# A transformer block: q, k and v of the second batch in seven block products for two token tiles, with weight sums kept from the first batch

## Chip, cores, metric

One core of a Trainium2 chip runs the whole program. The metric is device time in microseconds; the median of three runs of the kernel before is 3139.4 us.

## What is computed

One conditioned transformer block on `x` of 2 x 2048 x 576 in float32, 16 heads of 36, an MLP of 2304. A condition gives shifts, scales and gates. The change is in the lines that make q, k and v.

```python
mod = silu(c) @ w_ada + b_ada            # shifts, scales, gates
xn = ln(x, 1e-06) * (1 + sc_msa) + sh_msa
qkv = (xn @ w_qkv + b_qkv).reshape(B, N, 3, H, hd)
q, k = ln(q, 1e-05, qn_g, qn_b), ln(k, 1e-05, kn_g, kn_b)
attn = softmax(q @ k.T * hd ** -0.5)
x = x + g_msa * ((attn @ v) @ w_proj + b_proj)
xn2 = ln(x, 1e-06) * (1 + sc_mlp) + sh_mlp
x = x + g_mlp * (gelu(xn2 @ w1 + b1) @ w2 + b2)
```

## The kernel before

The two batches run one after the other: q, k, v of a batch, its attention, its output projection; the MLP of both stands last. A batch has 16 token tiles of 128 rows. A product on TensorE takes a tile's features as the stationary operand (128 x 128) and half of the columns of q, k or v (288) as the moving one. The 576 features are four full parts in float32 and a last part of 64, which is split into two rounded halves that lie one above the other and is multiplied in the faster fp32r form (the tail). Thus `product` (L1101, L1103) issues, per half, four f32 matmuls and two tail matmuls; the trace shows each f32 matmul as two records. A PSUM tile of pool `s` has two banks, one per half; there are four.

Around a tile's product, per batch, stand these steps:

- POOL loads a tile's rows (L984); DVE and ACT normalise them (L272 to L283, the root `std` L276 on ACT); DVE turns squares of 32 x 32 (L1000), and POOL stores them in four DMAs to a DRAM tile `turned` (L1005).
- POOL loads a tile's features back by column: `xnt` (L1013) and twice the last part (L1015). ACT scales and shifts them: four parts (L1022), the rounded last part (L388), the same unrounded as `tail` (L389); POOL subtracts (L390).
- DVE adds the bias while it empties PSUM (`biased`, L1115 for q and k, L1118 for v). ACT squares q and k (L1055), DVE sums by head (`var`, L1060), ACT takes the root (L1063), DVE inverts (L1065), POOL multiplies (`head_scale`, L1067).
- DVE turns q and k (L1080), and four DMAs write them by feature to DRAM `qk` (L1082, on SP's queue, near the end of a batch also on POOL's).
- For attention, key and query rows come back from `qk` (L812 `km`, L814 `ke`), and DVE scales and splits them (L847, L856, L857). Attention's products are L1245 and L1258, its exponential is L1249 on ACT.

On TensorE, DVE, POOL and SP instructions run in the order in which they are written in this part of the code; the order on ACT is made by a scheduler when the program is built. Every engine's queue is in order: an instruction that waits holds all behind it.

The first batch also makes the weights (`first_weights`): q's and k's columns are centred by head on DVE, the last 64 rows are split, and at tile `TPB + 1` `kept` stores them to DRAM on SP's queue, from where the second batch loads them (`kept_weights`).

## Time and profile before

| what | us |
|---|---|
| median of three runs (3139.19 to 3139.5) | 3139.4 |
| profiled execution, first to last instruction | 3137.1 |
| TensorE busy in it | 3113.8 |
| q, k, v of the second batch on TensorE | 1083.3 to 1295.07 |
| mean granted TensorE clock | 0.999 |

The profile is of one execution; for its own time the page gives the span alone, 2.3 us under the median of the runs. PE is TensorE, PEld its weight loads; DVE, ACT and POOL are the vector, scalar and GpSimd engines, SP the queue that mostly issues DMAs. A group's row names line, engine, operation, tiles and count, then total busy us and mean ns of one, then idle time ahead and what ended it. In a timeline row come start and length in us, and in brackets idle time and releaser. A windows row has the stretch, then busy us per engine with counts, then the granted clock, the DMA engines' share and GB/s.

### The profile page before, as it was taken

Reading aid. Unit: us, or ns where it says so; the run is one execution under the profiler, and the core shown is the slowest. Engines: PE = TensorE matmul, PEld = TensorE weight load, DVE = VectorE, ACT = ScalarE, POOL = GpSimd, SP = SyncE. Lnnn points to the kernel's source line nnn. Section 1 sums busy time; section 2 is a strip of 40 time slices with the busy share of each in tenths; the row PEclk is TensorE's granted clock in tenths of the full one; section 3 lists DMA queues with packets and bytes.
Section 4 is the critical chain, followed back from the end, with each engine's and each line's share of the span. In section 5 each row is a group of like instructions: output and inputs, shape, how many; then the busy total and the mean of one; then the engine's idle time right before and its main releaser. Section 6 shows DMA issues by size and latency. Waiting matters only on the chain.

```text
span 3137.1 us, 46798 instructions
## 1 busy us (share of the span) xinstructions
PE 3113.8 (99%) x17553; PEld 1859.8 (59%) x17553; DVE 1517.1 (48%) x2189; ACT 1472.4 (47%) x2847; POOL 664.8 (21%) x934
## 2 busy tenths in 40 slices
PE   8999999999999999999999999999999999999999
PEld 6883333333334788633333333368888888777777
DVE  6653434443444556444434444345565554545454
ACT  2326666666666132466666666633555541000000
POOL 4640000011110455200011210013333320111111
PEclk9999999999999999999999999999999999999999
DMA  5753221132221756411122321146554434333331
GB/s 147 178 106 85 78 66 46 56 82 68 66 73 53 239 101 123 86 44 35 47 57 73 86 66 56 57 167 191 159 142 132 128 110 166 106 121 121 113 106 39
DMA packets 300707, 311.94 MB, mean 99 GB/s; under 512 B 179192, under 2 KB 233336, under 8 KB 298360
## 3 DMA queue, kind: packets, MB, share of 16 engines
q1 hardware_dynamic: 252496, 192.19, 21.4%
q0 software_dynamic: 44432, 111.07, 13.4%
q10 hardware_dynamic: 3544, 5.60, 0.5%
q8 instruction: 141, 2.31, 0.3%
q14 instruction: 94, 0.77, 0.1%
HBM read 191.80 MB, written 106.45 MB: 95 GB/s over the span
## 4 chain that ended last, share of the span: by engine, by line
PE 98%; DVE 0%; issue 0%; DMA 0%; ACT 0%; POOL 0%; POOLq 0%; ACTq 0%
PE b L1258 29%; PE b L1245 20%; PE s L1833 16%; PE s L1101 12%; PE m L1673 12%; PE s L406 4%; PE m L1687 2%; PE one L1673 2%; PE s L1103 2%; PE s L417 0%; DMA xt<-x_dram 0%; PE b L192 0%; ACT xnt L395 0%; POOL x_dram L1400 0%; DVE wb L1602 0%
## 5 line engine op out<-in xcount | busy, mean ns | idle before, releaser
L1249 ACT ACTIVATE pt<-b 128x512 f32<-128x512 f32 x2048 | 1057.1, 609 | 482.0 <-PE b L1258 266.2
L1258 PE MATMUL b<-pt,vt 128*64 128x512 f32 x4096 | 935.0, 598 | 0.0
L1258 PEld LDWEIGHTS b<-pt,vt 128*64 128x64 f32 x4096 | 271.8, 136 | 582.1 <-issue 438.2
L1245 PE MATMUL b<-qm,km 32*128 32x512 f32 x4096 | 562.6, 613 | 0.0
L1310 DVE TENSOR_TENSOR ot<-b,ot 128x512 f32<-128x512 f32 x192 | 132.7, 691 | 618.6 <-PE b L1258 618.6
L1245 PE MATMUL b<-qe,ke 16*128 16x512 f32 x2048 | 419.3, 791 | 0.0
L1101 PE MATMUL s<-wq,xnt 128*128 128x288 f32 x1536 | 404.9, 407 | 2.0 <-ACT xnt L395 2.0
L1833 PE MATMUL s<-ws,as 128*128 128x288 f32 x1440 | 351.8, 406 | 0.0
L1245 PEld LDWEIGHTS b<-qm,km 32*128 32x128 f32 x4096 | 189.9, 184 | 270.7 <-ACT pt L1249 209.8
L1101 PEld LDWEIGHTS s<-wq,xnt 128*128 128x128 f32 x1536 | 281.7, 190 | 64.6 <-ACT xnt L395 1.6
L1833 PEld LDWEIGHTS s<-ws,as 128*128 128x128 f32 x1440 | 273.6, 190 | 75.6
L1277 DVE RECIPROCAL den<-den 128x512 f32<-128x512 f32 x64 | 213.6, 3337 | 10.6 <-DMA den<-den_dram 10.6
L1673 PE MATMUL m<-xnt,wb 128*128 128x256 f32 x864 | 210.3, 379 | 1.6 <-issue 0.9
L1673 PE MATMUL m<-s,wb 128*128 128x256 f32 x864 | 210.0, 379 | 0.0
L1005 POOL DMA_DIRECT2D turned<-squares x212 | 142.5, 679 | 261.3 <-DVE squares L1000 244.3
L1308 DVE COPY ot<-b 128x512 f32<-128x512 f32 x64 | 44.3, 691 | 278.2 <-PE b L1258 272.9
L1673 PEld LDWEIGHTS m<-s,wb 128*128 128x128 f32 x864 | 164.2, 190 | 22.3
L1245 PEld LDWEIGHTS b<-qe,ke 16*128 16x128 f32 x2048 | 106.1, 184 | 114.1 <-issue 113.4
L1673 PEld LDWEIGHTS m<-xnt,wb 128*128 128x128 f32 x864 | 158.9, 190 | 21.2 <-issue 1.3
L1711 ACT ACTIVATE cs<-cs,b_sb 128x512 f32<-128x512 f32 x144 | 98.8, 719 | 113.1 <-DVE cs L1706 88.7
L812 POOL DMA_DIRECT2D km<-qk x56 | 28.2, 503 | 571.7 <-PE b L1245 569.3
L1022 ACT ACTIVATE xnt<-xnt,mod 128x128 f32<-128x128 f32 x244 | 100.4, 481 | 98.9 <-DMA xnt<-turned 98.8
(206 smaller groups left out, 2942.1 us busy)
## 6 DMA issues: line engine op xcount, KB each, us to landing
gelu<-cs SPq DMA_DIRECT2D x144, 256.0 KB
hidden<-gelu SPq DMA_DIRECT2D x16, 2304.0 KB
x_dram<-spare POOLq DMA_DIRECT2D x64, 288.0 KB, 2.5
qm<-qk SPq DMA_DIRECT2D x256, 64.0 KB
den<-den_dram SPq DMA_DIRECT2D x128, 128.0 KB
turned<-squares POOLq DMA_DIRECT2D x212, 72.0 KB, 2.5
qk<-turned_qk SPq DMA_DIRECT2D x104, 144.0 KB
xnt<-turned POOLq DMA_DIRECT2D x54, 256.0 KB, 4.3
```

The source lines that it names most:

```text
L406: nc.tensor.matmul(outs[a], stationary(k, a), moving(k, a), start=(first and k == 0), stop=(not first and k == FULL - 1),)
L1005: queue.dma_start(out=by_square[g], in_=squares[g * SQ : (g + 1) * SQ, :].rearrange("p (k j) -> p k j", j=SQ))
L1022: nc.scalar.activation(part, part, AF.Identity, **affine(which, k, b))
L1101: nc.tensor.matmul(out_a, full[:, k, :], wq[:, k, f], start=k == 0, stop=False)
L1245: nc.tensor.matmul(ps, k[r, keys], q[r, :], start=first, stop=not first)
L1249: nc.scalar.activation(pt[:, h, :], banks[2 * c + h], AF.Exp, scale=SCALE)
L1258: nc.tensor.matmul(acc[64 * h : 64 * h + 64, :], vt[:, v0 : v0 + 64], pt[:, h, :], start=pt is pts[0][0], stop=pt is pts[-1][0],)
L1277: nc.vector.reciprocal(den, den)
L1310: nc.vector.tensor_tensor(ot, acc, ot, ALU.add)
L1673: nc.tensor.matmul(out_m[m], wb[:, slot[m], k, f * P : (f + 1) * P], moving[m](k), start=k == 0 and m in (1, 2, 5, 6), stop=k == 1 and m == 1,
L1711: nc.scalar.activation(part, part, AF.Gelu, bias=b1_sb[:, g : g + 1])
L1833: nc.tensor.matmul(ms[m], stationary[m][:, f, :], ws[m][:, f, :], start=(f == 0), stop=(f == HF - 1))
```

## The change

For the second batch, from its third tile on, two tiles (`t0`, `t0 + 1`) are multiplied together. Their features by two halves of the first 512 form a 2 x 2 block matrix, and so do the weights by two halves of the inputs and two of the columns; seven block products of sums replace eight. TensorE gets them in four groups, one PSUM tile each: a = (1), b = (2, 6), c = (5, 7), d = (4, 3). The tails stay eight; two matmuls of rows of ones with rows of bias (L1223) bring the bias in. ACT copies the first product to SBUF as `one` (L1233), and DVE makes the results in five additions that also empty PSUM (L1246 to L1250). POOL makes the three sums of the tokens' features with four additions (`token_sums`, L1260 to L1263). The four sums of weights and the difference of the two halves of the last rows are made on DVE in the first batch, one step per tile from the tile after `kept` on, stored by SP's queue, and loaded by it at the start of the second batch. The first two tiles of the second batch are done as before. Both tiles' features are now asked for together, once per pair, and the writing order of the whole stage is new (`in_pairs`).

Lines of the same steps in the new program: product L1136/L1138, bias L1150/L1153, row load L1013, stores L1034, feature loads L1042/L1044, modulation L1051, squares L1090, head scale L1095 to L1102, turned q and k L1115/L1117, attention's products L1489.

**ACT in the middle of the loop.** Before, for one tile and the next (`sq` squares, `var` and `std` roots, `xnt` modulations):

```order
L1063 ACTIVATE var_9611<-var_9611,eps5_67 128x32 [waits DVE_49]
L1055 ACTIVATE sq_9649<-both_9591 128x1152 [waits Activation_49]
L276 ACTIVATE std_9698<-mv_9696,eps6_65 128x1 [waits DVE_49]
L1022 ACTIVATE xnt_9659<-xnt_9659,mod_91 128x128 [waits DMASW6_49,PE_49]
L1022 ACTIVATE xnt_9659<-xnt_9659,mod_91 128x128 x3
L388 ACTIVATE xnt4_9660<-xnt4_9660,mod_91 128x128 [waits DMASW7_49,DMASW0_49,PE_49]
L389 ACTIVATE tail_9661<-xnt4_9660,mod_91 128x128 [waits Pool_49]
L1063 ACTIVATE var_9711<-var_9711,eps5_67 128x32 [waits DVE_49]
L1055 ACTIVATE sq_9745<-both_9691 128x1152 [waits Activation_49]
```

After, for one pair (`one` is the copy of a first product: of k, then q, then v):

```order
L1233 COPY one_9607<-s_9579 128x288 [waits PE_49]
L1098 ACTIVATE var_9560<-var_9560,eps5_67 128x32 [waits DVE_49]
L276 ACTIVATE std_9614<-mv_9612,eps6_65 128x1 [waits DVE_49]
L1051 ACTIVATE xnt_9567<-xnt_9567,mod_91 128x128 [waits DMASW3_49,Pool_49]
L1051 ACTIVATE xnt_9567<-xnt_9567,mod_91 128x128 x3
L388 ACTIVATE xnt4_9568<-xnt4_9568,mod_91 128x128 [waits DMASW5_49,DMASW4_49]
L389 ACTIVATE tail_9569<-xnt4_9568,mod_91 128x128 [waits Pool_49]
L1051 ACTIVATE xnt_9573<-xnt_9573,mod_91 128x128 [waits DMASW6_49]
L1051 ACTIVATE xnt_9573<-xnt_9573,mod_91 128x128 x3
L388 ACTIVATE xnt4_9574<-xnt4_9574,mod_91 128x128 [waits DMASW7_49,DMASW0_49]
L389 ACTIVATE tail_9575<-xnt4_9574,mod_91 128x128
L1233 COPY one_9697<-s_9669 128x288 [waits PE_49]
```

The modulations of two tiles stand in a row, and the copy of q's first product stands behind them. On POOL, the loads that these modulations wait for now stand behind both multiplies of the pair before:

```order
L1102 TENSOR_TENSOR pair_9359<-pair_9359,inv_9552 128x1152 [waits DVE_49]
L1102 TENSOR_TENSOR pair_9359<-pair_9359,inv_9563 128x1152 [waits DVE_49]
L1042 DMA xnt_9567<-turned25_9420 128x4x128 [waits DMASW4_49,DMASW3_49,PE_49]
L1044 DMA xnt4_9568<-turned25_9420 64x128 [waits PE_49]
L1044 DMA xnt4_9568<-turned25_9420 64x128 [waits DMASW5_49]
L1042 DMA xnt_9573<-turned26_9503 128x4x128 [waits DMASW7_49,DMASW6_49,DMASW0_49]
L1044 DMA xnt4_9574<-turned26_9503 64x128 x2
```

where before each tile's loads stood behind the multiply of one tile and the next row load:

```order
L1067 TENSOR_TENSOR both_9691<-both_9691,inv_9810 128x1152 [waits DVE_49]
L390 TENSOR_TENSOR xnt4_9756<-tail_9757,xnt4_9756 128x128 [waits DMASW7_49,DMASW0_49,Activation_49]
L984 DMA xt0_211<-in_x_dram 128x576 [waits DMASW5_49]
L1013 DMA xnt_9843<-turned29_9801 128x4x128 [waits DMASW3_49,DMASW4_49,DMASW2_49,DMASW6_49,DMASW1_49,PE_49]
L1015 DMA xnt4_9844<-turned29_9801 64x128 [waits PE_49,Pool_49]
L1015 DMA xnt4_9844<-turned29_9801 64x128
```

What moved: one multiply and the loads of one tile became two multiplies, then the loads of two tiles.

**TensorE in the same pair**, q's product; its third group is `s_9680`:

```order
L1221 MATMUL s_9669<-wq_8772,xnt_9360 128x288 [waits DVE_49,PE_49]
L1221 MATMUL s_9669<-wq_8772,xnt_9360 128x288
L1223 MATMUL s_9669<-bias_rows_9228,ones_9229 128x288
L1221 MATMUL s_9673<-wq_8772,xnt_9360 128x288 [waits DVE_49]
L1221 MATMUL s_9673<-wq_8772,xnt_9360 128x288
L1227 MATMUL s_9673<-wq4_8773,xnt4_9361 128x288 x2
L1221 MATMUL s_9673<-weight_sums_9147,more_9486 128x288 x2
L1221 MATMUL s_9680<-weight_sums_9147,more_9486 128x288 [waits Activation_49]
L1221 MATMUL s_9680<-weight_sums_9147,more_9486 128x288
L1223 MATMUL s_9680<-bias_rows_9228,ones_9229 128x288
```

The wait on Activation ahead of the third group is for the copy of the first one, whose PSUM tile it takes. Before, a product and the start of the next were:

```order
L1101 MATMUL s_9862<-wq_8754,xnt_9659 128x288 [waits DVE_49]
L1101 MATMUL s_9862<-wq_8754,xnt_9659 128x288 x3
L1103 MATMUL s_9862<-wq4_8755,xnt4_9660 128x288 x2
L1101 MATMUL s_9862<-wq_8754,xnt_9659 128x288 x4
L1103 MATMUL s_9862<-wq4_8755,xnt4_9660 128x288 x2
L1101 MATMUL s_9901<-wq_8754,xnt_9659 128x288 [waits DVE_49]
```

Nothing on TensorE waited for ACT there but for the features.

**POOL at the end of the stage.** Before (`km`, `ke` key rows; `qk` writes; the multiplies are of k of the last tile, then of q of the last two):

```order
L1067 TENSOR_TENSOR both_10443<-both_10443,inv_10460 128x576 [waits DVE_49,Pool_49]
L1082 DMA qk1_9128<-turned_qk_10466 32x18x32 [waits DVE_49]
L1082 DMA qk1_9128<-turned_qk_10466 32x18x32 x3
L1067 TENSOR_TENSOR both_10427<-both_10427,inv_10496 128x576 [waits DVE_49]
L1067 TENSOR_TENSOR both_10443<-both_10443,inv_10524 128x576 [waits DVE_49]
L812 DMA km1_10557<-qk1_9128 32x1024 [waits DMAHW4_49,DMAHW3_49,DMAHW5_49,DMAHW2_49,DMAHW6_49,DMAHW1_49,DMAHW7_49,DMAHW0_49,PE_49]
L814 DMA ke1_220<-qk1_9128 16x1x1024 [waits DMASW5_49]
```

After:

```order
L812 DMA km1_10765<-qk1_9146 32x1024 [waits DMAHW4_49,DMAHW3_49,DMAHW5_49,DMAHW2_49,DMAHW6_49,DMAHW1_49,DMAHW7_49,DMAHW0_49,PE_49]
L814 DMA ke1_220<-qk1_9146 16x1x1024
L812 DMA km1_10765<-qk1_9146 32x1024
L814 DMA ke1_220<-qk1_9146 16x1x1024
L1117 DMA qk1_9146<-turned_qk_10673 32x18x32 [waits DVE_49]
L1117 DMA qk1_9146<-turned_qk_10673 32x18x32 x3
L1102 TENSOR_TENSOR pair_10565<-pair_10565,inv_10723 128x576 [waits DVE_49]
L1102 TENSOR_TENSOR pair_10565<-pair_10565,inv_10730 128x576 [waits DVE_49]
```

Four key loads, which wait for the last v product, moved ahead of the writes and of both multiplies of q.

The diff's core:

```diff
+            def sum_made(i):
+                for k in range(2):
+                    one, other = (
+                        (block(0, 1), block(0, 0)),
+                        (block(1, 1), sums[:, 0]),
+                        (block(1, 1), block(0, 1)),
+                        (sums[:, 1], block(1, 0)),
+                    )[i]
+                    nc.vector.tensor_tensor(sums[:, i, k], one[:, k], other[:, k], ALU.subtract)
...
+            def sums_kept():
+                saved["sums"] = dram.tile([P, 4, 2, 3, HALF], F32, name="sums_kept")
...
-                turned_qk = work.tile([P, 2 * C], F32, name="turned_qk", bufs=3)
+                turned_qk = work.tile([P, 2 * C], F32, name="turned_qk", bufs=3 - b)
...
+                nc.gpsimd.memset(ones[0:2, :].bitcast(F32), 1.0)
...
+                factors = {
+                    1: (a11, by_block(0, 0)),
+                    2: (a12, by_block(1, 0)),
+                    3: (more[:, 2], by_block(1, 1)),
+                    4: (a22, by_sum(3)),
+                    5: (more[:, 0], by_sum(0)),
+                    6: (more[:, 1], by_sum(1)),
+                    7: (s3, by_sum(2)),
+                }
+                tails = {2: (0, tail(0)), 3: (0, tail(1)), 4: (1, less[:, w, :]), 7: (1, tail(1))}
+                out = {}
+                for group in ((1,), (2, 6), (5, 7), (4, 3)):
+                    ps = s_tile()
+                    for a, m in enumerate(group):
+                        out[m] = ps[:, a, :HALF]
+                        out[group] = ps[:, :, :HALF]
+                        x_, w_ = factors[m]
+                        for k in range(2):
+                            nc.tensor.matmul(out[m], x_[:, k, :], w_(k), start=k == 0, stop=k == 1 and m == 6)
+                        if m in (1, 5):
+                            nc.tensor.matmul(out[m], ones, spread[:, w, int(m == 5), :], start=False, stop=True)
+                        if m in tails:
+                            i, w_ = tails[m]
+                            for j in range(2):
+                                nc.tensor.matmul(out[m], parts[i][:, j, :], w_, start=False, stop=j == 1)
...
+                one = work.tile([P, HALF], F32, name="one", bufs=2)
+                nc.scalar.copy(one, out[1])
...
+                tt = nc.vector.tensor_tensor
+                return [
+                    lambda: tt(dst(both_t, 0), two(out[2, 6]), spread_over(single(one)), ALU.add),
+                    lambda: tt(dst(both_t, 1), two(out[5, 7]), spread_over(dst(1, 0)), ALU.add),
+                    lambda: tt(dst(1, 0), dst(1, 1), single(out[4]), ALU.subtract),
+                    lambda: tt(dst(1, 1), dst(1, 1), single(out[5]), ALU.add),
+                    lambda: tt(dst(0, 1), dst(0, 1), single(out[3]), ALU.add),
+                ]
...
+            def token_sums(t0):
+                a, c = xnts[t0][0], xnts[t0 + 1][0]
+                more = work.tile([P, 3, 2, P], F32, name="more", bufs=2)
+                tt = nc.gpsimd.tensor_tensor
+                tt(more[:, 0], c[:, 0:2, :], c[:, 2:4, :], ALU.add)
+                tt(more[:, 1], more[:, 0], a[:, 0:2, :], ALU.subtract)
+                tt(c[:, 0:2, :], a[:, 0:2, :], c[:, 0:2, :], ALU.subtract)
+                tt(more[:, 2], a[:, 2:4, :], more[:, 1], ALU.subtract)
+                return more
+            def row_begun(t):
...
+                    xnts[t] = input_loaded(turned.pop(t), nc.gpsimd, work if t % 4 == 3 else None)
...
+            def in_pairs():
+                sums = work.tile([P, 4, 2, 3, HALF], F32, name="weight_sums")
+                less = work.tile([P, 3, HALF], F32R, name="wq4_less")
+                nc.sync.dma_start(out=sums, in_=saved["sums"])
+                nc.sync.dma_start(out=less.bitcast(F32), in_=saved["less"])
+                row_begun(4)
+                row_begun(5)
+                pairs[0] = work.tile([P, 2, 2 * C], F32, name="pair", bufs=2)
+                both.update((t, pairs[0][:, t, :]) for t in range(2))
+                for t in range(2):
+                    input_modulated(b, xnts[t + 1])
+                    features_begun(t + 2) if t + 2 not in xnts else None
+                    q, k = product(0, t), product(1, t)
+                    biased(0, q, t)
+                    turn_begun(t + 3)
+                    biased(1, k, t)
+                    if t == 1:
+                        turn_begun(5)
+                        row_begun(6)
+                        row_begun(7)
+                    if t > 0:
+                        head_scale(t - 1)
+                    v = product(2, t)
+                    biased(2, v, t)
+                    squared(t)
+                    if t == 0:
+                        spread, ones = bias_rows()
+                input_modulated(b, xnts[3])
+                more = token_sums(2)
+                for t0 in range(2, NT, 2):
+                    last = t0 == NT - 2
+                    operands = sums, less, spread, ones, more
+                    pairs[t0] = work.tile([P, 2, 2 * C], F32, name="pair", bufs=2)
+                    for t in range(2):
+                        both[t0 + t] = pairs[t0][:, t, :]
+                        features_begun(t0 + 2 + t)
+                    out = seven_products(1, t0, operands)
+                    do = combined(1, t0, out)
+                    if t0 == 2:
+                        head_scale(1)
+                    turn_begun(t0 + 4)
+                    do[0]()
+                    by_feature(t0 - 2, ready=not last)
+                    do[1]()
+                    by_feature(t0 - 1, ready=not last)
+                    do[2](), do[3](), do[4]()
+                    if not last:
+                        for t in range(2):
+                            input_modulated(b, xnts[t0 + 2 + t])
+                    if last:
+                        squared(t0, 1, 2)
+                        squared(t0 + 1, 1, 2)
+                    out = seven_products(0, t0, operands)
+                    do = combined(0, t0, out)
+                    if not last:
+                        more = token_sums(t0 + 2)
+                        turn_begun(t0 + 5)
+                        row_begun(t0 + 6)
+                        row_begun(t0 + 7)
+                        for i in range(5):
+                            do[i]()
+                        squared(t0)
+                        out = seven_products(2, t0, operands)
+                        do = combined(2, t0, out)
+                        do[0]()
+                        do[1]()
+                        head_scale(t0)
+                        squared(t0 + 1)
+                        do[2](), do[3](), do[4]()
+                        head_scale(t0 + 1)
+                        continue
+                    head_scale(t0, 1, 2)
+                    do[0]()
+                    head_scale(t0 + 1, 1, 2)
+                    do[1]()
+                    by_feature(t0, 1, 2, ready=False)
+                    do[2](), do[3](), do[4]()
+                    by_feature(t0 + 1, 1, 2, ready=False, queue=nc.gpsimd)
+                    for t in range(2):
+                        squared(t0 + t, 0, 1)
+                    key_rows = [*taken]
+                    for ready in key_rows[:-2]:
+                        ready()
+                    out = seven_products(2, t0, operands)
+                    do = combined(2, t0, out)
+                    head_scale(t0, 0, 1)
+                    do[0]()
+                    head_scale(t0 + 1, 0, 1)
+                    do[1]()
+                    by_feature(t0, 0, 1, ready=False)
+                    do[2](), do[3](), do[4]()
+                    by_feature(t0 + 1, 0, 1, ready=False)
+                    return key_rows[-2:]
...
+            if b > 0:
+                return in_pairs()
...
+                if b == 0 and t > TPB + 1 and summed:
+                    summed.pop(0)()
```

More of the change, by code (lines that the diff above doesn't have):

```diff
@@ L966, in kept @@
                 nc.sync.dma_start(out=saved["wq4"], in_=wq4.bitcast(F32))
-            return (wq, wq4, bq), close, (made, ends_made, bias_made, bias_spread, kept)
+            summed = [*(lambda i=i: sum_made(i) for i in range(4)), ends_less, sums_kept]
+            return (wq, wq4, bq), close, (made, ends_made, bias_made, bias_spread, kept, summed)
         def kept_weights():
@@ L1141, in inputs @@
             if b == 0:
[L1142 removed]
+                made, ends_made, bias_made, bias_spread, kept, summed = making
                 done, modulated = 3, {0, 1, 2}
```

76 lines of the change are left out of this document (68 added, 8 removed).

## The prediction

> **What bounds the kernel now.** I read the page first (busy shares, the chain that ended last), then the stretch in which the second batch's q, k and v are made: its groups of instructions and its table by windows.
>
> ```profile
> PE 3113.8 (99%) x17553; PEld 1859.8 (59%) x17553; DVE 1517.1 (48%) x2189; ACT 1472.4 (47%) x2847; POOL 664.8 (21%) x934
> PE 98%; DVE 0%; issue 0%; DMA 0%; ACT 0%; POOL 0%; POOLq 0%; ACTq 0%
> ...
> L1101 PE MATMUL s<-wq,xnt 128*128 128x288 f32 x768 | 201.9, 406 | 0.0
> L1103 PE MATMUL s<-wq,xnt 128*128 128x288 f32 x192 | 61.7, 402 | 0.0
> ...
> 1120.00:1160.00 40.00, 40.00 (x184) 32.34 (x182) 23.20 (x37) 12.16 (x27) 23.07 (x31) 1.00 0.60 114
> ```
>
> TensorE is 98% of the chain. The two rows in the middle are all of the stage (1083.3 to 1295.07 us): 96 half products, each of 8 records of the f32 lines (two records make one matmul) and 2 of the tail line. TensorE waits for nothing there, so 211.8 / 96 = 2.205 us for a half product. In the windows row TensorE is busy all 40 us, DVE 23.2, ACT 12.2, POOL 23.1. So matmuls taken out are time taken out, as long as what must be made per pair keeps to the shorter beat.
>
> **What is removed and added on TensorE.** A pure f32 stretch of the MLP gives the f32 price:
>
> ```profile
> 2899.80 16.90 PE L1833 MATMUL s<-ws,as 128*128 128x288 f32 x69
> 2916.53 8.65 PE L1833 MATMUL s<-ws,hidden 128*128 128x288 f32 x35
> 1286.16 2.10 PE L1101 MATMUL s<-wq,xnt 128*128 128x288 f32 x8
> 1287.88 0.64 PE L1103 MATMUL s<-wq,xnt 128*128 128x288 f32 x2
> 1288.36 2.10 PE L1101 MATMUL s<-wq,xnt 128*128 128x288 f32 x8
> ```
>
> 16.73 us / 69 = 0.2425 a record, 0.485 a matmul; a tail matmul is then (2.205 - 8 x 0.2425) / 2 = 0.1325. Two tiles of one of q, k, v take four half products now: 16 f32 and 8 tail matmuls, 8.82 us. The seven products take 14 f32, 8 tail and 2 bias matmuls: 14 x 0.485 + 10 x 0.1325 = 8.12. That saves 0.70, for 3 weights x 7 pairs (the first two tiles stay as they were): **-14.6 us**. The starts of the last three rows would split it otherwise (1.72 / 8 = 0.215, 0.48 / 2 = 0.24), which saves 0.38 x 21 = 8.0. I take the first, since 69 records in a row say more than eight; 8.0 is kept as the other end.
> The four groups of a product, in order: a (first product and bias) 1.10, b 2.21, c 2.34, d 2.47.
>
> **What lies beside.** In the first batch eleven subtractions on DVE over five tiles, two or three for a tile of 6 x 2.205 = 13.2 us; the nearest row (752 ns for 576 elements, below) makes 864 about 1.1, so 2.2 to 3.3 us where DVE has 42% idle: 0. Four MB go out and come back on SP's queue; the sums are needed 2 x 13.2 = 26.5 us after they are asked for, and where they came later they would hide in the wait that comes next: 0. Making the bias rows (eighteen short DVE instructions) stands early in the first of these tiles: 0, its cover being the same.
>
> **The loop of pairs.** Durations:
>
> ```profile
> L1067 POOL TENSOR_TENSOR both<-both,inv 128x1152 f32<-128x1152 f32 x13 | 27.6, 2126 | 14.7 <-DVE inv L1065 14.7
> L1115 DVE TENSOR_TENSOR both<-s,bq 128x576 f32<-128x576 f32 x24 | 18.0, 752 | 29.1 <-PE s L1103 29.1
> L1060 DVE TENSOR_REDUCE var<-sq 128x32 f32<-128x1152 f32 x13 | 17.4, 1339 | 0.0
> L272 DVE BATCH_NORM_STATS2 st<-xt 128x6 f32<-128x288 f32 x14 | 5.7, 445 | 0.0
> L1065 DVE RECIPROCAL inv<-var 128x32 f32<-128x32 f32 x13 | 4.6, 353 | 5.0 <-ACT var L1063 5.0
> L1063 ACT ACTIVATE var<-var,eps 128x32 f32<-128x32 f32 x13 | 4.2, 321 | 45.9 <-DVE var L1060 45.9
> xnt<-turned POOLq DMA_DIRECT2D x11, 256.0 KB, 4.9
> DMA to landing us min/median/max: 3.3/4.3/5.9
> ...
> 1181.81 1.65 ACT L1022 ACTIVATE xnt<-xnt,mod 128x128 f32<-128x128 f32 x4 [6.68 <-DMA xnt<-turned]
> 1183.36 0.48 ACT L388 ACTIVATE xnt<-xnt,mod 128x128 fp32r<-128x128 f32 x1
> 1183.75 0.48 ACT L389 ACTIVATE tail<-xnt,mod 128x128 f32<-128x128 f32 x1
> ```
>
> In the new order, group c of q goes into the PSUM tile that group a of the same product left, and ACT empties it (the copy `one`). That copy stands in ACT's queue behind the twelve modulations of the next two feature tiles; those wait for the feature loads, which POOL issues only behind both head-scale multiplies of the pair before. I count from V, when the v product of the pair before ends. Its group c is ready at V - 2.47; DVE then adds (0.75), reduces (1.34), ACT takes the root (0.32), DVE inverts (0.35), does three single adds (3 x 0.445, by the 288-element row), reduces again (1.34), root and inverse (0.67): V + 3.6, with some 0.3 for hops V + 3.9. POOL multiplies (2.13): V + 6.0. The loads land 4.9 later: V + 10.9. Six modulations took 2.42 us in the last rows, so twelve, at their pitch, 4.75: V + 15.7; the copy (0.5; between 0.48 for 128 elements here and the 0.75 of DVE) V + 16.2. TensorE gets there at V + 8.12 + 1.10 + 2.21 = V + 11.4. **It waits 4.7 us**, in each of the five pairs that have a next one to modulate (tiles 4, 6, 8, 10, 12): **+23.5**. With landings of 3.3 and 5.9 it is 3.1 and 5.7: 15.5 to 28.5. Nothing shortens this by itself, since V of the next pair moves along.
>
> **The first pair.**
>
> ```profile
> L1005 POOL DMA_DIRECT2D turned<-squares x42 | 28.2, 678 | 49.4 <-DVE squares L1000 47.9 <-issue 1.5
> L390 POOL TENSOR_TENSOR xnt<-tail,xnt 128x128 fp32r<-128x128 f32 x12 | 5.5, 458 | 4.2 <-ACT tail L389 4.2
> L1000 DVE STREAM_TRANSPOSE squares<-xt 128x576 f32<-128x576 f32 x7 | 5.4, 778 | 0.2
> L283 DVE TENSOR_SCALAR xt<-xt,mv,rstd 128x576 f32<-128x576 f32 x7 | 4.1, 579 | 0.3
> L984 POOL DMA_DIRECT2D xt<-in_x_dram x6 | 3.8, 633 | 0.0
> L276 ACT ACTIVATE std<-mv,eps 128x1 f32<-128x1 f32 x10 | 2.9, 293 | 48.5 <-DVE mv L274 48.5
> ```
>
> The sums of the first pair's tokens (two adds on POOL before the sixth product can start) stand behind a row tile's way to DRAM, and that row's root stands on ACT behind the copy of this pair's group a. From the end of a: copy 0.5, root 0.29, inverse 0.2, normalise 0.58, transpose 0.78, four stores 2.7, two row loads 1.27, multiply 2.13, tail 0.46, two adds of 256 elements (between 458 ns for 128 and the multiply's; 0.65 each) 1.3: 10.2. TensorE has the second product to do meanwhile, 1.24. **+9.0** (7 if the stores were covered half, 9.5 with hops).
>
> **Into attention.**
>
> ```profile
> 1286.19 2.70 POOL L1082 DMA_DIRECT2D qk<-turned_qk  x4 [4.40 <-DVE turned_qk L1080]
> 1290.11 1.16 POOL L1067 TENSOR_TENSOR both<-both,inv 128x576 f32<-128x576 f32 x1 [1.21 <-DVE inv L1065]
> 1292.78 0.78 DVE L1080 STREAM_TRANSPOSE turned_qk<-both 128x576 f32<-128x576 f32 x1
> 1295.07 0.31 PEld L1245 LDWEIGHTS b<-qm,km 32*128 32x128 f32 x8 [0.17 <-DVE turned_qk L1080]
> 1295.17 0.55 POOL L812 DMA_DIRECT2D km<-qk  x1 [1.11 <-PE s L1103]
> 1295.72 0.62 POOL L814 DMA_DIRECT2D ke<-qk  x1
> 1295.97 0.47 DVE L847 TENSOR_SCALAR km<-km,gb_at 64x256 f32<-64x256 f32 x1
> ```
>
> Now POOL's key loads wait for the last v matmul but stand last. In the new order four of them stand ahead of the four stores and of both q multiplies; the transpose of q waits for the first multiply, and DVE's last adds of v, which free attention's second bank, stand behind it. From the last matmul: 2.34 + 2.70 + 1.16 + 0.78 + 0.445 + 0.47 + 0.445 = 8.3, less the 0.17 there is now: **+8.2**. If DVE ran past the transpose it would be 0.
>
> **The clock.** Seven new gaps may cost more than their length.
>
> ```profile
> 17.61 0.55 PE L230 MATMUL s<-ident,rows 128*128 128x128 f32 x3 [0.64 <-DVE rows L222]
> 19.11 5.81 PE L1101 MATMUL s<-wq,xnt 128*128 128x288 f32 x16 [0.95 <-ACT xnt L395]
> 24.54 0.91 PE L1103 MATMUL s<-wq,xnt 128*128 128x288 f32 x4
> 18.00:20.00 2.00, 1.05 (x5) 0.74 (x4) 1.41 (x10) 1.48 (x4) 1.38 (x5) 0.89 1.05 291
> 20.00:24.00 4.00, 4.00 (x11) 2.89 (x11) 2.48 (x6) 1.23 (x4) 0.98 (x2) 0.63 1.08 371
> ```
>
> Behind gaps of 0.64 and 0.95 us at the start the granted clock falls to 0.89 and 0.63 in these windows, and sixteen records take 5.43 instead of 16 x 0.2425 = 3.88: 1.55 lost. Seven gaps cost between 0 and 10.9. It is one instance, so I take 1 us each: **+7**. The Trainium skill, page "TensorE: Matmul & The Clock Gate", section "Part 1: The HAM clock gate (the "warmup" mystery)", says the gate halves the clock after a whole idle window of about 3.4 us on a free-running grid. By that page a gap of 4.7 us holds a whole window about 4 times in 10, the two long ones always, so that the term would be, as an estimate, about 6; the drop above came behind less idle time than the rule asks for.
>
> **The sum** on the profiled span: 3137.1 - 14.6 + 9.0 + 23.5 + 8.2 + 7 = 3170.2. The median of the runs, 3139.4, lies 2.3 above that span: **3172 us**.
>
> **Rivals.**
> - *POOL's queue does not carry the waits* (faster). If its DMA issues ran beside its multiplies, the feature loads would start at V and be hidden, the first pair would wait 9.0 - 2.7 - 1.27 - 2.13 = 2.9 and attention 8.2 - 5.0 = 3.2: 3139.4 - 14.6 + 6.1 = 3131. It decides from the point where the gaps sum to less than 8.3. Against it: the first row of the transition charges POOL 2.70 for four stores, and key loads follow each other at 0.55. Chance 0.08.
> - *The loop holds, the two single waits stay*: 3139.4 - 14.6 + 17.2 + 2 = 3144, no change that can be told. It needs landings below 0.2 us or the copy ahead of the modulations. 0.05.
> - *The transition is covered*: 3172 - 9 = 3163. DVE would have to be late less than the q multiplies. 0.15.
> - *Longer*: landings of 5.9 and the full clock price, 3172 + 5 + 4 = 3181; the two feature tiles now load in one burst, which speaks for it. With the smaller saving, 3188. 0.20.
> - The forecast itself, 3157 to 3179: 0.52.
>
> 0.2% (6.3 us) is what a measurement of this kernel can tell from no change; from the cases: faster 0.08, within it 0.05, slower 0.87. The range reaches from the shortest landings without the transition's wait and without a clock price (3139.4 - 14.6 + 9.0 + 15.5 = 3149) to the longest with the smaller saving, 3188.
>
> **What would show it.** In the trace after: a product of two tiles 8.1 us long; TensorE idle 4 to 5 us five times, released by ACT's copy, with ACT waiting for the feature loads ahead of it; one idle time of about 9 us at the first pair, released by POOL's sums; one of about 8 at the first attention matmul, released by DVE. Granted clock near 0.5 behind some of them. I am wrong if ACT's copy stands ready at V + 11, or if feature loads start before the second multiply has ended.

## The result, and the profile after

The changed kernel takes 3177.3 us (median of four runs, 3174.57 to 3177.69) beside 3139.45 us for the kernel before on the same chip: ratio 1.0119, 95% interval 1.0105 to 1.0133, 37.9 us slower. Its profiled execution spans 3175.0 us, 2.3 under its median as before. The forecast was 3172 with a range of 3149 to 3188.

The page's line of busy times and instructions:

```profile
PE 3114.0 (98%) x17511; PEld 1857.9 (59%) x17511; DVE 1571.6 (49%) x2277; ACT 1479.8 (47%) x2868; POOL 684.7 (22%) x965
```

TensorE is as busy as before (3113.8) with 42 fewer records. So the work taken out is hidden in this line: matmuls at half clock count as longer busy time (27.6 us of it, see below). The waits of TensorE from 40 to 1345 us show the new ones (what waits, on what, us in total, times, longest):

```profile
PE s L1221 <- ACT one L1233: 16.1, 5, 4.3
PE s L1221 <- POOL more L1261: 9.2, 1, 9.2
PE b L1489 <- issue: 7.3, 1, 7.3
PE s L1136 <- ACT xnt L1051: 4.1, 1, 4.1
```

The timeline of TensorE has their places; the second and third rows are the starts of one and the next weight's product of the same pair:

```profile
1127.27 3.87 PE L1221 MATMUL s<-weight_sums,more 128*128 128x288 f32 x8 [9.15 <-POOL more L1261]
1134.80 1.13 PE L1221 MATMUL s<-wq,xnt 128*128 128x288 f32 x4
1142.91 1.13 PE L1221 MATMUL s<-wq,xnt 128*128 128x288 f32 x4
1165.41 2.29 PE L1221 MATMUL s<-weight_sums,more 128*128 128x288 f32 x4 [2.81 <-ACT one L1233]
...
1283.28 1.37 PE L1221 MATMUL s<-weight_sums,more 128*128 128x288 f32 x4 [4.26 <-ACT one L1233]
1330.76 1.55 PE L1489 MATMUL b<-qm,km 32*128 32x512 f32 x3 [7.26 <-issue]
```

An undisturbed product of two tiles takes 1142.91 - 1134.80 = 8.11 us, as forecast (8.12). The stage now runs from 1089.14 to 1322.38 us, 233.24 us long where it was 211.77. Attention's first two matmuls start at 1322.38 and its third at 1330.76.

POOL ahead of the first pair's sixth product, whose wait ends at 1127.27: a head-scale multiply and, behind it, the second of the token sums.

```profile
1123.19 2.14 POOL L1102 TENSOR_TENSOR pair<-pair,inv 128x1152 f32<-128x1152 f32 x1
...
1126.49 0.72 POOL L1261 TENSOR_TENSOR more<-more,xnt 128x256 f32<-128x256 f32 x1
```

POOL and DVE ahead of attention's third matmul: four stores, the two multiplies of q, then the transpose that waits for the first of them, and the addition whose end (1330.66) lies 0.1 us before that matmul:

```profile
1324.71 2.67 POOL L1117 DMA_DIRECT2D qk<-turned_qk  x4
1327.40 2.27 POOL L1102 TENSOR_TENSOR pair<-pair,inv 128x576 f32<-128x576 f32 x2
1328.60 0.78 DVE L1115 STREAM_TRANSPOSE turned_qk<-pair 128x576 f32<-128x576 f32 x1 [2.67 <-POOL pair L1102]
...
1330.20 0.46 DVE L1249 TENSOR_TENSOR vt<-vt,s 128x288 f32<-128x288 f32 x1
```

One pair of the loop, from the head-scale multiplies of the pair before to the product that waits:

```profile
1243.78 2.13 POOL L1102 TENSOR_TENSOR pair<-pair,inv 128x1152 f32<-128x1152 f32 x1 [1.04 <-DVE inv L1100]
1245.85 0.79 POOL L1042 DMA_DIRECT2D xnt<-turned  x1
...
1249.36 1.65 ACT L1051 ACTIVATE xnt<-xnt,mod 128x128 f32<-128x128 f32 x4 [4.41 <-DMA xnt<-turned]
1253.60 0.48 ACT L389 ACTIVATE tail<-xnt,mod 128x128 f32<-128x128 f32 x1
1253.99 0.38 ACT L1233 COPY one<-s 128x288 f32<-128x288 f32 x1
...
1254.42 1.24 PE L1221 MATMUL s<-weight_sums,more 128*128 128x288 f32 x4 [2.80 <-ACT one L1233]
```

The reader sees the chain of the forecast link by link: POOL issues the feature loads only behind the second multiply, ACT waits 4.41 us for them, and the copy that empties group a's PSUM tile stands behind the last modulation.

### The profile page after: what moved, and what is told of

Same layout as the page of the kernel before. It is cut to its first block, busy times and chain, and to the rows that moved or that the text cites. A ratio compares the mean times of both kernels' runs of the same rounds, so it can differ in the third digit from the quotient of the medians.

```text
span 3175.0 us, 46895 instructions
## 1 busy us (share of the span) xinstructions
PE 3114.0 (98%) x17511; PEld 1857.9 (59%) x17511; DVE 1571.6 (49%) x2277; ACT 1479.8 (47%) x2868; POOL 684.7 (22%) x965
## 5 line engine op out<-in xcount | busy, mean ns | idle before, releaser
L1489 PE MATMUL b<-qm,km 32*128 32x512 f32 x4096 | 565.1, 615 | 7.3 <-issue 7.3
L1489 PE MATMUL b<-qe,ke 16*128 16x512 f32 x2048 | 421.8, 793 | 0.0
L1489 PEld LDWEIGHTS b<-qm,km 32*128 32x128 f32 x4096 | 192.0, 185 | 277.8 <-ACT pt L1493 208.7
L1136 PE MATMUL s<-wq,xnt 128*128 128x288 f32 x864 | 228.6, 409 | 6.5 <-ACT xnt L1051 4.1
L1034 POOL DMA_DIRECT2D turned<-squares x212 | 142.3, 678 | 219.7 <-DVE squares L1029 204.0
L1136 PEld LDWEIGHTS s<-wq,xnt 128*128 128x128 f32 x864 | 158.9, 191 | 43.1 <-ACT xnt L1051 4.3
L1489 PEld LDWEIGHTS b<-qe,ke 16*128 16x128 f32 x2048 | 107.9, 184 | 114.0 <-issue 113.2
L1051 ACT ACTIVATE xnt<-xnt,mod 128x128 f32<-128x128 f32 x244 | 100.5, 481 | 144.3 <-DMA xnt<-turned 128.2
```

Of the source, the lines that this page charges most:

```text
L1034: queue.dma_start(out=by_square[g], in_=squares[g * SQ : (g + 1) * SQ, :].rearrange("p (k j) -> p k j", j=SQ))
L1051: nc.scalar.activation(part, part, AF.Identity, **affine(which, k, b))
L1136: nc.tensor.matmul(out_a, full[:, k, :], wq[:, k, f], start=k == 0, stop=False)
L1489: nc.tensor.matmul(ps, k[r, keys], q[r, :], start=first, stop=not first)
```

## Where the clock went

The windows view in stretches of 3.413 us (TensorE's busy time and count, then the granted clock, DMA share, GB/s), each with the one that follows it:

```profile
1161.38:1164.79 3.41, 1.22 (x6) 1.00 1.08 153
1164.79:1168.20 3.41, 2.79 (x6) 0.50 0.92 136
1250.12:1253.53 3.41, 1.50 (x8) 1.00 1.09 166
1253.53:1256.94 3.41, 2.52 (x12) 1.00 0.92 136
```

Half clock begins on a fixed grid of 3.413 us: the next two times are at 1195.51 and 1226.23 us, 9 and 18 stretches behind 1164.79. A stretch with 2.19 us idle (busy 1.22) is followed by one at half clock; the one with 1.91 us idle (busy 1.50) is not. Behind the wait at 1165.41 a second stretch was at half clock too, with TensorE busy 6.2 us in the two. So a loop wait of 2.7 to 4.3 us costs up to 3.1 us more, or nothing (the one at 1254.42), by where it falls on the grid. Added over the trace, TensorE was busy 27.6 us at half clock behind seven of the eight new waits, which is 13.8 us lost.

These two stretches are not the whole rule. In the traces of all the kernels of this document, of the stretches at full clock between 40 us and the second batch's attention, each of the 32 with 2.01 us idle or more was followed by half clock, and of the 27 with 1.3 to 1.92 us idle one was, in the last kernel below. In the first 9 us of attention, four stretches with 1.3 to 1.7 us idle were followed by it too; why less was enough there is not shown.

## The experiments

**The store in quarters.** Four stores of a quarter each, one behind each sum, instead of one of all four:

```diff
+  if i == 0:
+      saved["sums"] = dram.tile([P, 4, 2, 3, HALF], F32, name="sums_kept")
+  nc.sync.dma_start(out=saved["sums"][:, i], in_=sums[:, i])
...
-  nc.sync.dma_start(out=saved["sums"], in_=sums)
```

> The weight sums are stored in four DMAs, each right behind its two subtractions (tiles 6 to 9), instead of one DMA of 3.5 MB at tile 11; DVE's work is the same. Theory (the big store delays the small stores of row tiles, which landed 12.6 us after issue instead of 2.6, so that the last tile's features come late): the wait of 4.1 us at 219 us and the half clock behind it (1.7) go, 3171.5 us, and the stores of row tiles land within 5 us. Rival (DVE's subtractions, 2 us each instead of the 1.1 I took, push the rows late): the wait stays, 3177 us.

3168.9 us, ratio 1.0093 (1.0076 to 1.0110). The DMA issues from 186 to 206 us of the changed kernel, and then of this one (KB each, median us to landing):

```profile
sums_kept<-weight_sums SPq DMA_DIRECT2D x1, 3456.0 KB
...
turned<-squares POOLq DMA_DIRECT2D x4, 72.0 KB, 12.6
```

```profile
turned<-squares POOLq DMA_DIRECT2D x8, 72.0 KB, 3.2
```

Behind the store of 3.4 MB, the small stores of a row tile land after 12.6 us instead of 3.2 (and after 4.1 from 100 to 190 us, where the quarters travel); the features loaded from them then come late, and TensorE waits 4.1 us in the first batch. In quarters that wait is gone, while the loop's five (15.2 us) and the other two stay. The time fell by 8.4, more than the wait and its half clock (4.1 + 1.6): the loop's waits also fall elsewhere on the clock's grid, and half clock behind all the other waits takes 9.8 us where it took 12.1.

**The features ahead.** The loads of the next pair's features, written behind q's product (so ahead of the head-scale multiplies on POOL):

```diff
-  features_begun(t0 + 2 + t)
+  if t0 == 2:
+      features_begun(t0 + 2 + t)
...
+  for t in range(2):
+      features_begun(t0 + 4 + t)
```

> In the loop of pairs the feature loads of the next pair are issued on POOL ahead of both head-scale multiplies instead of behind them; nothing else. Theory (q's third group waits for ACT's copy, the copy for the modulations, these for loads that stand behind the multiplies): the five waits on the copy, 16.1 us in sum, go, and with them half-clock time worth about 8; the multiplies end 3.7 us later, so that DVE's transposes hold k's additions and up to 7 us of new waits on DVE may come: 3153 to 3162 us. Rival (the copy is late for another reason, such as its own place in ACT's queue alone): the waits on the copy stay within 1 us of what they are, 3177 us.

3164.5 us, ratio 1.0081 (1.0064 to 1.0098), 2.5 above the expected range; its profiled execution spans 3158.8. The five waits on ACT are gone, but the longest new one shows what is late next (TensorE's timeline):

```profile
1193.59 2.26 PE L1221 MATMUL s<-weight_sums,xnt 128*128 128x288 f32 x4 [6.19 <-DVE pair L1249]
```

POOL's queue was the cause of the late features; moving the loads up hands part of the time to DVE's additions (6.19 here, 1.89 in one more).

**The first pair's sums ahead.** The modulation of tile 3 and the sums of its pair, written ahead of the row work of tile 1:

```diff
+  input_modulated(b, xnts[3])
+  more = token_sums(2)
   turn_begun(5)
...
-  input_modulated(b, xnts[3])
-  more = token_sums(2)
```

> The token sums of the first pair (and the modulation they need) are written ahead of the fifth tile's way to DRAM, the row loads and the first head-scale multiply. Theory (the 9.2 us wait of the sixth product is the queue on POOL ahead of the sums): it goes, with 1.7 us of half clock; what was ahead now comes later, and some 5 us of new waits on ACT and DVE may follow in the same pair: 3166 to 3172 us. Rival (the sums wait for their data, not for their place): the 9.2 us stay, 3177 us.

3170.65 us, ratio 1.0099 (1.0082 to 1.0116). The wait on POOL falls from 9.2 to 1.7 us; in the same pair waits on DVE of 2.3 and 0.5 and one on ACT's copy of 0.5 come instead. The place was right; of the 7.5 us, 3.3 came back.

**The key loads on SP.** The eight loads of the second pair of heads' keys, four of which stand ahead of the stores on POOL's queue, issued by SP:

```diff
-  rows_taken(nc.gpsimd, m, e, ...)
+  rows_taken(nc.sync if b and p == 1 else nc.gpsimd, m, e, ...)
```

> The eight loads of the second pair of heads' keys, four of which stand on POOL ahead of the last stores and of q's multiplies, go to SP's queue in the second batch; nothing else. Theory of the prediction (the way into attention is POOL's queue): the wait before attention falls from 8.4 us by 2.3 or more, as the four loads leave it, 3172 to 3174 us. Rival (DVE's own queue is as late: key scaling, two reductions, v's additions one after another): it falls by 1.1 us or less, 3176 us.

3173.6 us, ratio 1.0108 (1.0091 to 1.0125); the wait ahead of attention is 4.9 us instead of 7.3. So the key loads on POOL carry 2.4 us of it. The rest is no longer POOL's: the four stores are now issued from 1318.37 us, before the last v product ends, and DVE works from 1322.12 to 1326.73 with one pause of 0.4 us (additions of v, a reduction, an inverse, a transpose, a scaling of keys), 0.1 us before attention's third matmul starts.

**k's additions ahead.** DVE's five additions of k in one piece, ahead of the transposes of the pair before:

```diff
-  do[0]()
+  for i in range(5):
+      do[i]()
   by_feature(t0 - 2, ready=not last)
-  do[1]()
   by_feature(t0 - 1, ready=not last)
...
-  do[2](), do[3](), do[4]()
```

> In the loop DVE's five additions for k are written ahead of the two transposes of the pair before, which wait for POOL's multiplies; the feature loads stay where they are, behind the multiplies. Theory (the wait is of a PSUM tile: q's third group gets the tile of its own first group because k's tiles come free late; with k's additions ahead it gets one of k's): the five waits on ACT's copy go although the modulations are as late as before, some 7 us of waits under 1.5 us each take their place (v's second group on ACT's copy and DVE), and no half clock: 3177 - 16 - 8 + 7 = 3160 us. Rival (whatever the tile, TensorE has to wait for the late features): 3175 us or more.

3156.9 us, ratio 1.0059 (1.0043 to 1.0074), the largest step of one edit. The same chain of features and copy stands in its timeline, no earlier, yet TensorE no longer waits for it:

```profile
1184.58 1.65 ACT L1051 ACTIVATE xnt<-xnt,mod 128x128 f32<-128x128 f32 x4 [4.35 <-DMA xnt<-turned]
1189.22 0.37 ACT L1233 COPY one<-s 128x288 f32<-128x288 f32 x1
```

```profile
1185.43 2.10 PE L1221 MATMUL s<-weight_sums,more 128*128 128x288 f32 x8
1187.15 0.51 PE L1223 MATMUL s<-bias_rows,ones 128*128 128x288 f32 x1
1191.20 1.13 PE L1221 MATMUL s<-wq,xnt 128*128 128x288 f32 x4
```

v's product begins at 1191.20, so q's began 8.11 us earlier, at 1183.09. The eight records from 1185.43 close its group b and open group c, which is at its bias matmul at 1187.15, 2.1 us before the copy of group a (1189.22) that held it in the changed kernel. So q's group c has another tile than the one that group a leaves, k's tiles being empty sooner. The waits on ACT fall from 16.1 to 2.7 us (five of 0.5). So the late features cost time only through the tile that the copy frees.

**Work in the gaps.** 18 spare matmuls at the first pair and 5 in each loop wait; they add nothing to the results:

```diff
+  for _ in range(spare_products):
+      nc.tensor.matmul(out[m], a12[:, 0, :], wq[:, 0, half[0]], start=True, stop=True)
```

> Spare f32 matmuls, whose results are overwritten, are put ahead of the sixth product: 18 (8.7 us) in the first pair's k and 5 (2.4 us) in q of the pairs with a late copy, so that TensorE works through most of the waits it had; nothing comes ready sooner. Theory (idle TensorE time of some 2 us within one 3.41 us window brings half clock for the next): the waits shrink by the spare matmuls' length, the half clock behind those six waits goes, 9.8 us by the trace of the changed kernel: 3167 to 3170 us. Rival (the time lost behind the waits is not the clock, or only a whole idle window brings it): the windows behind the short waits cost the same as before, 3177 us.

3170.8 us, ratio 1.0101 (1.0086 to 1.0117): 6.5 us back, just short of what the clock theory asked for. Two windows that had a granted clock of 0.94 in the changed kernel (TensorE busy 26.12 and 26.83 us) read full clock (same columns as above):

```profile
1195.00:1225.00 30.00, 28.78 (x133) 1.00 0.61 112
1225.00:1255.00 30.00, 29.16 (x136) 1.00 0.63 120
```

The gaps' results come no sooner, only their clock price goes: no half clock is left behind the six filled gaps, where it took 9.8 us. The wait ahead of attention, not filled here, grew from 7.3 to 8.7, and half clock there and in the first batch by 1.2 us, which is most of what is missing.

**All places at once.** The quarters, the first sums, k's additions, and v's five additions ahead of the key rows and of q's last head scales:

```diff
-  for ready in key_rows[:-2]:
-      ready()
   out = seven_products(2, t0, operands)
   do = combined(2, t0, out)
...
+  for ready in key_rows[:-2]:
+      ready()
+  for i in range(5):
+      do[i]()
   head_scale(t0, 0, 1)
...
```

> All places mended: weight sums stored in four parts, first token sums ahead, k's additions ahead of the transposes, and in the last pair v's additions ahead of the last head scales of q. Theory: of the 39 us between the changed kernel and the sum without waits (3139.3 - 14.6 = 3124.7) there remain 3 us in the first pair, 7 in the loop, 4 to 6 into attention and at most 2 of half clock: 3139 to 3143 us. Rival (the seven products save less than 14.6, or the waits only move): 3150 us or more.

3148.2 us, ratio 1.0029 (1.0017 to 1.0042), 5 above the expected range. Two rows of ACT and TensorE where attention begins:

```profile
1297.88 1.47 PE L1487 MATMUL b<-qm,km 32*128 32x512 f32 x3 [2.67 <-issue]
1298.48 0.31 ACT L1099 ACTIVATE var<-var,eps 128x16 f32<-128x16 f32 x1 [5.82 <-DVE var L1096]
```

q's last roots now come after attention has begun, on ACT ahead of its exponentials, and the clock is 0.50 from 1298 to 1303 us and 0.55 to 1308, with TensorE busy all the while: 4.8 us lost, where at most 2 were expected. In neither of the two orders that were run did the seventh pair's work end before attention began.

**The last pair by eight.** The changed kernel, its last two tiles multiplied one by one as before:

```diff
-  for t0 in range(2, NT, 2):
+  for t0 in range(2, NT - 2, 2):
...
-      return in_pairs()
+      in_pairs()
-  for t in range(NT - 2):
+  for t in range(NT - 2) if b == 0 else ():
...
```

> The changed kernel, with the last two token tiles of the second batch made by eight products again, tile by tile, in the order that the kernel before has at that place; six pairs keep seven products. One theory: the 8.4 us by which the attention starts late come from the last pair's own order (its key loads stand behind five GpSimd operations of the recombination), and its wait at 1283 us (4.3 us) goes with the pair. Then 8.4 and 4.3 us of waits go, some 4 us of half clock behind them, and 2.1 us of the saving (14.6 / 7) are given back: 3177.3 - 8.4 - 4.3 - 4 + 2.1 = about 3163 us, between 3160 and 3168, and no wait of over 2 us ahead of the attention. Rival: the attention waits wherever the pairs end, since GpSimd and VectorE have fallen behind by then: a wait of over 5 us stays ahead of the attention, and the time is 3173 us or more.

3172.6 us, ratio 1.0105 (1.0089 to 1.0120): some 10 us above what I expected. I had two things wrong. The wait at 1283 us belongs to pair 12, which stays: the waits on ACT are still 15.9 us in five. And the wait ahead of attention went, but one inside it took its place:

```profile
PE b L1483 <- ACT pt L1474: 4.5, 1, 4.5
```

**Six pairs, all mends.** The quarters, the first sums, k's additions, and this tail, in one kernel (edits as above).

> The store of the sums in quarters, the first pair's sums ahead, k's additions ahead of the transposes, and the last two tiles by eight products, all in one kernel. Theory: nothing is left that TensorE waits for but some 3 us at the first pair and some 5 us in the loop, without the late roots that the kernel with all places mended still had ahead of its attention. Its 3148.2 us lose then a wait of 2.7 us, some 3 us of half clock and 2 to 4 us of late start, and take back 2.1 us: 3139 to 3144 us, level with the kernel before to within 0.2%. Rival: the pairs' GpSimd and VectorE work is late in any order, so a wait of 3 us or more turns up elsewhere with half a clock window behind it: 3147 us or more. To win clearly it would have to come in under 3133 us, which neither expects.

3147.7 us, ratio 1.0022 (1.0013 to 1.0031): the rival's number, above the expected 3139 to 3144. The wait inside attention is here too; the rows of ACT, POOL and TensorE ahead of it:

```profile
1298.91 4.27 ACT L1473 ACTIVATE pt<-b 128x512 f32<-128x512 f32 x8 [4.96 <-PE b L1469]
...
1306.99 0.11 POOL L771 MEMSET spare<- 1x11 f32 x1 [4.79 <-DMA qm<-qk]
1307.13 0.53 ACTq L1811 DMA_DIRECT2D spare<-in_w_dram  x1
1307.70 1.09 ACT L1473 ACTIVATE pt<-b 128x512 f32<-128x512 f32 x2 [4.52 <-DMA qm<-qk]
1308.35 5.82 PE L1482 MATMUL b<-pt,vt 128*64 128x512 f32 x16 [3.76 <-ACT pt L1473]
```

The profile names the query rows' loads as the releaser of the ninth exponential. But between the eighth and the ninth ACT's queue has a DMA into `spare`, and POOL's memset of that tile ends just ahead of it. In the kernel before sixteen exponentials stand ahead of this DMA; here ACT's scheduler put it behind eight.

**That DMA off ACT.** One word changed, so that GpSimd issues it:

```diff
-  nc.scalar.dma_start(out=last_rows, in_=w1[512:576, :].rearrange("p (a f) -> p a f", a=2))
+  nc.gpsimd.dma_start(out=last_rows, in_=w1[512:576, :].rearrange("p (a f) -> p a f", a=2))
```

> The kernel of six pairs and all mends, with one DMA of 576 KB (the last rows of the MLP's weights into the tile spare) issued by GpSimd instead of ACT; ACT's other work, and all else, stays in its order. In the kernel before ACT has sixteen exponentials of the attention ahead of that issue, in the kernel of six pairs eight. Theory: the 3.8 us that TensorE waits 11 us into the attention (row at 1308.35) are ACT held at that issue, which waits for the tile to come free; with it go the wait and the half clock behind it (granted clock 0.77 over 1300 to 1315 us, 3.4 us): 3147.7 - 3.8 - 3.4 = 3140.5, between 3138 and 3143. Rival: the exponentials wait for query rows whose loads land late, and the issue only stands beside that: the wait stays at over 3 us and the time at 3146 us or more.

3139.6 us (11 runs) beside 3139.2 (21 runs), ratio 1.0003 (0.9994 to 1.0012): 8.0 us for that word, and the kernel before is reached. The waits of TensorE that the view lists between 40 and 1345 us:

```profile
PE s L1222 <- DVE pair L1247: 4.0, 2, 2.4
PE s L1222 <- ACT one L1234: 3.1, 6, 0.5
PE s L1222 <- POOL more L1262: 1.3, 1, 1.3
```

The wait of 3.8 us inside attention is not among them. The exponentials were held by the issue, not by the query rows.

**Row tiles behind.** Normalising and transposing of the next row tiles behind the first addition of k and of q, instead of ahead (shown for k):

```diff
+  do[0]()
   turn_begun(t0 + 4)
-  for i in range(5):
+  for i in range(1, 5):
       do[i]()
...
```

> As the kernel with the DMA on GpSimd, with the next row tiles' normalising and transposing written behind the first of the five additions of k and of q on VectorE, instead of ahead of it. Theory: the 2.3 and 1.6 us of waits on the first addition (rows at 1128.34 and 1191.22 of the kernel of six pairs) go, with half a clock window behind the first (1.5 us), and small waits of 0.2 to 0.6 us come in their place: 3 to 5 us less than the kernel with the DMA on GpSimd alone, 3134 to 3139 us, at most level with the kernel before and perhaps 0.1% faster. Rival: VectorE is late by its own sum of work there, so what is moved behind makes the second addition or the next pair wait as long: less than 1.5 us of gain.

3139.0 us (11 runs), ratio 0.9999 (0.9990 to 1.0008): 0.7 us less than without it, which these runs can't tell from nothing: the rival's case. The waits on the first addition went; others came:

```profile
1114.58 2.21 PE L1222 MATMUL s<-weight_sums,more 128*128 128x288 f32 x8 [1.65 <-POOL more L1262]
1128.17 1.77 PE L1222 MATMUL s<-weight_sums,xnt 128*128 128x288 f32 x4 [1.91 <-DVE pair L1250]
1158.51 1.24 PE L1222 MATMUL s<-wq,xnt 128*128 128x288 f32 x4 [0.54 <-ACT one L1234]
1183.64 1.24 PE L1222 MATMUL s<-wq,xnt 128*128 128x288 f32 x4 [0.54 <-ACT one L1234]
...
1295.46 1.18 PE L1471 MATMUL b<-qm,km 32*128 32x512 f32 x3 [1.64 <-DMA qk<-turned_qk]
```

Its stretches of the clock's grid at the two ends (columns as above):

```profile
1125.27:1128.68 3.41, 1.50 (x8) 1.00 0.23 82
1128.68:1132.09 3.41, 3.41 (x10) 0.50 0.70 92
1292.52:1295.93 3.41, 1.77 (x8) 1.00 0.86 165
1295.93:1299.34 3.41, 3.41 (x24) 0.50 1.04 216
```

Here 1.91 us idle (busy 1.50) is followed by half clock, where the same busy time was not in the changed kernel.

A pair of the loop takes 1183.64 - 1158.51 = 25.13 us: three products of 8.11 and 0.80 for a wait of 0.54 with its restart. Two tiles one by one took 12 x 2.205 = 26.46. So each pair in the loop does gain, 1.33 us net. Over six pairs that is 8.0, and the two ends take it back: 1.65 and 1.91 us at the first pair, 1.64 at attention, and 1.7 of half clock at each, 8.6 in all. The stage's own length bears this out: its first product starts at 1084.00 and attention at 1292.70, 208.7 us where it was 211.77, and what that saves is lost again where attention starts. (This execution spans 3139.2 us, 2.1 more than the one of the kernel before.)

## Why the prediction was right, and where not

The direction and the mechanism held. The sum came near by luck: the loop was priced 7.4 us too high and the clock 6.8 too low. By the prediction's steps:

| term | forecast us | measured us |
|---|---|---|
| saving on TensorE | -14.6 | 21 x (8.11 - 8.82) = -14.9 |
| first pair | +9.0 | 9.15 |
| loop of pairs, five waits | +23.5 | 16.1 |
| into attention | +8.2 | 1330.76 - 1322.38 = 8.4, idle 7.3 of it |
| clock | +7 | 13.8 |
| stores and loads of the sums | 0 | 4.1 |
| sum | 33.1 | 36.6 of 37.9 |

- *TensorE*: the price from the long f32 stretch was right, not the other end (8.0); 0.70 x 21 is 14.7, not 14.6.
- *The first pair and into attention*: POOL's rows above stand in the forecast order, and the multiply (2.13 us forecast, 2.14 measured) and the four stores (2.70 and 2.67) have the forecast lengths. The wait came at attention's third matmul, not its first; the view names no releaser, and DVE's addition ending 0.1 us before it, in two kernels, is what speaks for DVE.
- *The loop*: the chain is the one shown above; the features ahead and k's additions ahead each took hold of a link of it. What was off is mainly one size, the landing of the feature loads: I took 4.9 us, the median of the old stage; with 3.5 the same working gives 5 x 3.3 = 16.5. The DMA issues of the changed kernel from 1130 to 1290 us:

```profile
xnt<-turned POOLq DMA_DIRECT2D x11, 256.0 KB, 3.5
```

- *The clock*: seven gaps at 1 us each was half of it. The Trainium skill, page "TensorE: Matmul & The Clock Gate", section "Part 1: The HAM clock gate (the "warmup" mystery)", asks for a whole idle window of about 3.4 us on a free-running grid. The grid agrees (3.413 us here); the whole idle window does not: 2.19 us idle of 3.41 was enough, and the half clock behind the wholly idle stretches alone is 1.6 + 1.7 + 2.4 = 5.7 us of the 13.8.
- *The failed step* is "Four MB go out and come back on SP's queue": I counted when the sums are needed, and not what else travels beside a store of 3.4 MB. It delayed the small stores of a row tile from 3.2 to 12.6 us. DVE's subtractions, which I also costed at nothing, took 17.3 us, not 8 x 1.1 = 8.8, but the quarters kept them and the wait went, so they had cover. The price was right for half of them (shortest, median and longest in ns, first and last start):

```profile
L961 DVE TENSOR_TENSOR weight_sums<-wq,weight_sums x2: 1046/2174/3302, 139.1 to 142.3; 128x864 f32<-128x864 f32 x2
```

The one at 139.1 took 3.30 us beside POOL's multiply (138.90 to 141.04), the one at 142.3, behind it, 1.05. It is so in all four steps: 2.59 to 3.89 us for the first beside a multiply, 1.05 to 1.30 for the second. That the multiply is the cause was not tested.
- *Rivals*: "the loop holds" failed as it stood, since the landings were 3.5 and the copy stayed behind the modulations; k's additions ahead made it true by another way, the tile. "The transition is covered" failed: 8.4 us stayed. That POOL's queue carries the waits was right in the loop, and for a third of the wait ahead of attention; with the key loads on SP, DVE's queue keeps the rest.

What stays open: 1.3 us of the 37.9; why some stretches of the clock's grid with less than 2 us idle brought half clock and others did not; and why the wait ahead of attention is 7.3 us in some of these kernels and 8.7 in others. Whether a still shorter chain of the first pair would bring the six pairs under the kernel before was not tried.

## What to carry to other kernels

Work taken from the engine that bounds is worth what its neighbours' queues let through: here seven products do shorten the loop, and a longer chain at each end of the loop (first features in, last keys out) gives about as much back. Price a wait by the instruction that stands ahead of the releaser on its in-order queue and by the buffer that it frees, then change the one that is cheap to change: the order of five additions was worth 20 us, moving one DMA issue 8. And add the clock's price, up to 3.1 us here, to each gap of 2 us or more on TensorE.

## What was not expected of the hardware

- Half clock after 2.01 us idle or more within a 3.413 us stretch, 32 times of 32; after 1.3 to 1.92 us once in 27 ahead of attention; and a stretch at half clock with 0.6 us idle was followed by another (from 1164.79 us).
- While a store of 3.4 MB travels, stores of 72 KB from another queue land after 12.6 us instead of 3.2.
- An issue of a DMA on ACT that waits for its tile held exponentials for 3.8 us, and the profile gave another releaser.
- A subtraction of 864 elements on DVE took 1.05 to 1.30 us alone and 2.59 to 3.89 beside a multiply on POOL.
